# Gate and up projections of a second ffn: eight products of tiles, or seven of quarters' sums for pairs of tiles

## The chip, the cores and the metric

The kernel runs on one core of a Trainium2 chip. The metric is the device time of one execution in microseconds, as the median of several runs. TensorE does the matmuls into PSUM, VectorE (DVE), ScalarE (ACT) and GpSimd (POOL) do the rest, and transfers are issued from two queues, that of SyncE (SP) and that of GpSimd.

## The reference

Two layers over an input of 2 x 512 x 512 in float32. The first layer multiplies an autocorrelation attention with the SiLU of a first ffn. The second layer multiplies a state-space mixer (128 heads, an input projection of some 18,600 columns) with the SiLU of a second ffn. Each layer adds its product to its input. The second ffn is what the change is about; its weights are int4 values with a scale for each group of 128:

```python
def _L1_ffn_ref(x, gate_q, gate_s, up_q, up_s, down_q, down_s):   # H = 512, I = 1792, G = 128
    Wg = dequant(gate_q, gate_s)
    Wu = dequant(up_q, up_s)
    Wd = dequant(down_q, down_s)
    gate_score = jax.nn.silu(jnp.einsum('bsh,ih->bsi', x, Wg))
    intermediate = gate_score * jnp.einsum('bsh,ih->bsi', x, Wu)
    return jnp.einsum('bsi,hi->bsh', intermediate, Wd)
```

The `x` of it is the layer norm of the first layer's output, `xn1T` in the kernel (transposed, one tile of 128 x 4 x 512 for each of the two batches). The mixer also needs, ahead of its main loop, the decays of all heads (softplus, cumulated sums, exponentials) and the output projection's weights times the norm's weights.

## The kernel before, in words

The kernel has three parts in time: the first layer (to about 245 us), the second ffn (to about 574 us), and the mixer with the final products (to the end). The first layer's instructions are placed by a scheduler; from the second ffn on (`tc.manual_schedule()`) each engine runs what the program issues in the order it is written.

The second ffn goes through the 1792 inner columns in four blocks of 512, 512, 512 and 256 (`blocks`). The weights of a block come by two transfers each for gate, up and down (the values `q` and the broadcast scales `w`), and VectorE multiplies the two (`dequant`, L503) into one of six tiles of a ring. For each batch `b` and each tile `i` of 128 inner columns, TensorE makes `pg` and `pu` (L721): four matmuls of 128 x 128 weights with 128 x 512 columns for each of the two, added up over the 512 input features in one PSUM bank. A float32 matmul is two instructions in the trace, so eight for `pg` and eight for `pu`. ScalarE takes the SiLU of `pg` into `it` (L729), VectorE multiplies it by `pu` (L730). After the tiles of a batch the down projection follows, `pf` (L752), four row tiles of 128 with one matmul for each of the block's tiles, which VectorE adds into `gl` (L760, L762).

Between these tiles the program issues, one step at a time, two generators. `prepare` (`pieces`) makes what the mixer needs: loads of its small inputs, the root of the mean square (ScalarE's squares L567), `hn` and its transposes `ht` into `hT` (L580, L581), the projection `pdt` (L593), a softplus by a series on VectorE (L614 to L625), `Af` and its two parts (L628 to L636), and the sums `cs`, `cj`, `ct` by TensorE (L642 to L667), which go to memory as `cs_d`, `ea_d` and `sl_d`. `scale_out` (`scaled`) takes the output projection's weights through the core: a load of 512 KB into one of two tiles `wop` (L688, SP's queue), two multiplications by `gn` on VectorE (L697), a store to `wo_d` (L700, GpSimd's queue). A step loads piece i and scales piece i - 1:

```python
for i in range(len(pieces) + 1):
    if i < len(pieces):
        ts[i] = tmp.tile([P, WOP, D], F32, tag="wop", name=f"wop{i}", bufs=2)
        nc.sync.dma_start(ts[i], ...)
    if i > 0:
        ...                      # two tensor_scalar of 128 x 512
        nc.gpsimd.dma_start(wo_d[g][:, k : k + WOP, :], t)
    yield
```

PSUM has six banks for the second ffn's products (`bank`, tag `mm`), given out in turn, and two for transposes.

The mixer already makes its gates in another way (`Gates`, L1035 to L1107): for two tiles together, from quarters of the weights and of `hT`, by seven products of 128 x 128 with 128 x 256 for what would be eight. It needs sums of quarters of the columns (`th`, made by GpSimd once for each batch, L607) and of the weights (`sw`, L1055), and the results come together in PSUM halves and by ScalarE's copies and VectorE's additions. Steps for which `plain` is true make their gates by whole tiles (`gate`, L1026).

Of the kernel before, what the change touches and what calls it, by code (L numbers as in the profile page):

```python
# [8 lines left out]
F32 = mybir.dt.float32  # L9
# [6 lines left out]
P = 128  # L16
D = 512
# [25 lines left out]

WOP = 2
# [6 lines left out]
def fused_kernel(  # L51
# [412 lines left out]
    def hquarters(b):  # L464

        return [
            hT[:, 2 * k : 2 * k + 2, b * S + j * HD : b * S + j * HD + HD]
            for k in range(2)
            for j in range(2)
        ]  # L470
# [21 lines left out]
    with ExitStack() as l1:  # L492
# [33 lines left out]
        def prepare():  # L526
# [27 lines left out]
            for b in range(B):  # L554
# [48 lines left out]

                b11, b12, b21, b22 = hquarters(b)
                t1, t2, t3, t4 = (th[:, b, i] for i in range(4))
                for dst, p, q_ in ((t1, b12, b11), (t2, b22, t1), (t3, b22, b12), (t4, b21, t2)):
                    nc.gpsimd.tensor_tensor(dst, p, q_, ALU.subtract)  # L607
# [54 lines left out]
                csT = row("csT", "csT", (P, 2, S))  # L662
                eaT = row("eaT", "eaT", (P, 2, S))
                for j, a in enumerate((Ah, Al)):
                    ps = bank(f"ct{b}{j}")
                    for r in range(NCH):
                        nc.tensor.matmul(  # L667
                            ps[:, bass.ts(r, P)], a[:, r, :], upper, start=True, stop=True
                        )
                    nc.vector.tensor_copy(csT[:, j, :], ps)  # L670
                    nc.scalar.activation(eaT[:, j, :], ps, AF.Exp)
                nc.sync.dma_start(cs_d[b], csT[:, 0, :])
                for j in range(2):
                    nc.sync.dma_start(ea_d[j, b], eaT[:, j, :])
# [4 lines left out]
        def scale_out():  # L679

            pieces = [divmod(i, GT) for i in range(0, NG * GT, WOP)]
            ts = {}
            for i in range(len(pieces) + 1):
                if i < len(pieces):
                    g, k = pieces[i]
                    ts[i] = tmp.tile([P, WOP, D], F32, tag="wop", name=f"wop{i}", bufs=2)
                    o0 = g * GW + k * P
                    nc.sync.dma_start(  # L688
                        ts[i],
                        out_wT[o0 : o0 + WOP * P, :].rearrange("(k p) o -> p k o", p=P),  # L690
                    )
                if i > 0:
                    g, k = pieces[i - 1]
                    t = ts.pop(i - 1)
                    for j in range(WOP):
                        ct = g * GT + k + j
                        nc.vector.tensor_scalar(  # L697
                            t[:, j, :], t[:, j, :], gn[:, ct : ct + 1], None, ALU.mult
                        )
                    nc.gpsimd.dma_start(wo_d[g][:, k : k + WOP, :], t)  # L700
                yield
# [4 lines left out]
        ]  # L706
        fin = {kind: load_block(kind, 0) for kind in "gud"}
        w = {"g": fin["g"](), "u": fin["u"]()}
        pieces, scaled = prepare(), scale_out()
        for n, (i0, iw) in enumerate(blocks):  # L710
# [3 lines left out]
            for b in range(B):  # L714
                its = []
                for i in range(ni):
                    ps = {}
                    for kind in "gu":
                        ps[kind] = bank(f"p{kind}{i0}{i}{b}")
                        for k in range(KD):  # L720
                            nc.tensor.matmul(  # L721
                                ps[kind],
                                w[kind][:, k, bass.ts(i, P)],
                                xn1T[b][:, k, :],
                                start=(k == 0),
                                stop=(k == KD - 1),
                            )
                    it = hand.tile([P, S], F32, tag=f"h{4 * b + i}", name=f"it{i0}{b}{i}")
                    nc.scalar.activation(it, ps["g"], AF.Silu)  # L729
                    nc.vector.tensor_tensor(it, it, ps["u"], ALU.mult)  # L730
                    its.append(it)
                    if b == 0 and i == (2 if n == 0 else 0):
# [3 lines left out]
                    if b == 1 and i == 0 and more:  # L736
                        nxt["g"] = nxt["g"]()
                        nxt["u"] = load_block("u", n + 1)
                    if b == 1 and i == ni - 1 and more:
                        nxt["u"] = nxt["u"]()  # L740
                        fin["d"] = load_block("d", n + 1)
                    if n > 0 or b > 0:
                        next(pieces, None)
                        next(scaled, None)
                if n == 0 and b == 0:
                    wh = {q: load_hid(q) for q in range(2)}
                    wbc = {0: load_bc(0)}
                for r in range(NCH):
                    rt = b * NCH + r
                    po = bank(f"pf{i0}{rt}")  # L750
                    for i in range(ni):
                        nc.tensor.matmul(  # L752
                            po,
                            its[i][:, bass.ts(r, P)],
                            w["d"][:, i, :],
# [10 lines left out]
                    if r % 2 == 1 and (n > 0 or b > 0):  # L766
                        next(pieces, None)
                    if n > 0 or b > 0:
                        next(scaled, None)
            w.update(nxt)  # L770
# [13 lines left out]
    with ExitStack() as sm:  # L784
# [250 lines left out]
        class Gates:  # L1035
# [4 lines left out]
            def __init__(self, s):  # L1040
# [3 lines left out]
                a11, a12, a21, a22 = (  # L1044
                    w[:, 2 * k : 2 * k + 2, bass.ts(r, P)] for r in range(2) for k in range(2)
                )
                sw = wk.tile([P, 4, 2, P], F32, tag="sw", name=f"sw{s}", bufs=1)
                s1, s2, s3, s4 = (sw[:, i] for i in range(4))
                for dst, x, y, op in (
                    (s1, a21, a22, ALU.add),  # L1050
                    (s2, s1, a11, ALU.subtract),
                    (s3, a11, a21, ALU.subtract),
                    (s4, a12, s2, ALU.subtract),
                ):
                    nc.gpsimd.tensor_tensor(dst, x, y, op)  # L1055
                b11, b12, b21, b22 = hquarters(b)
                t1, t2, t3, t4 = (th[:, b, i] for i in range(4))
                self.factors = {
                    1: (a11, b11),
                    2: (a12, b21),  # L1060
                    3: (s4, b22),
                    4: (a22, t4),
                    5: (s1, t1),
                    6: (s2, t2),
                    7: (s3, t3),
                }

            def multiply(self, *which):
                for i in which:
# [7 lines left out]
                    x, y = self.factors[i]  # L1077
                    for k in range(2):
                        nc.tensor.matmul(  # L1079
                            ps,  # L1080
                            x[:, k, :],
                            y[:, k, :],
                            start=(i in (1, 2) and k == 0),
                            stop=(k == 1),
                            skip_group_check=True,
                        )
# [229 lines left out]
        def step(d):  # L1316
# [149 lines left out]
            else:  # L1466
# [12 lines left out]
                hcd = [values(s, px) for s, px in zip(n[:1], pxs)]  # L1479
# [3 lines left out]
                hcd += [values(s, px) for s, px in zip(n[1:], pxs[1:])]  # L1483
# [6 lines left out]
                if plain(d):  # L1490
                    held = [gate(a[0], "pj")]
# [179 lines left out]
```

## Time and profile before

| | |
|---|---|
| median of 7 runs | 2325.96 us (2323.52 to 2329.19) |
| the profiled execution | 2327.99 us, its span 2326.2 us, granted TensorE clock 0.992 |
| PE busy | 2273.7 us (98%) |
| DVE, ACT, POOL busy | 1406.7, 1222.6, 1067.3 us |
| second ffn, 272 to 574 us: PE, DVE, ACT, POOL busy | 296.63, 131.48, 54.87, 31.59 us of 302 |
| `pg`, `pu`, `pf` | 101.8, 100.7, 99.7 us busy, 224 instructions each |

A group's line gives the source line, the engine, the operation, written and read tiles, shapes and count; then busy us and mean ns of one; then the idle time of the engine just before the group and what ended it. A matmul's busy time is modelled and overlaps its neighbours (its mean is 592 to 599 ns for 512 columns, where one starts every 429 ns), so the pace of TensorE is read from stretches of the chain or the timeline, not from the mean. In the timeline a line gives start and length in us of a run of like instructions, and in brackets the idle time before it and its releaser.

### The profile page before, as it was taken

The numbers are of one execution on the slowest core, as the hardware profiler recorded it, in microseconds if no ns is written. First come the engines' busy times: TensorE is split into PE (matmuls) and PEld (weight loads), VectorE is DVE, ScalarE is ACT, GpSimd is POOL, SyncE is SP. The second block draws the span as 40 slices with busy tenths as digits, with TensorE's granted clock in tenths as the row PEclk, the third lists the DMA queues.
The fourth block names the chain that finished last, engine by engine and source line by source line (L and its number), as shares of the span: only waits on it lengthen the run. The fifth ranks groups of instructions, "written<-read, shape, count | busy, mean of one in ns | idle before, by whom it ended". The sixth has DMA issues, their size and how long they took to land.

```text
span 2326.2 us, 32436 instructions
## 1 busy us (share of the span) xinstructions
PE 2273.7 (98%) x11516; PEld 1547.3 (67%) x11516; DVE 1406.7 (60%) x2672; ACT 1222.6 (53%) x2605; POOL 1067.3 (46%) x907
## 2 busy tenths in 40 slices
PE   7989999999999999999999999999999999999998
PEld 4545444544557777777777777777777777777776
DVE  5263436632666666666667666666666676756663
ACT  3141112111676666666666575666666665657560
POOL 4151201100164554745554474447465654645475
PEclk9999999999999999999999999999999999999999
DMA  4012356762454444434544354545445454544452
GB/s 165 0 57 70 99 166 226 257 236 82 132 169 138 143 138 154 123 123 139 184 135 128 118 159 136 145 154 146 118 128 168 130 156 127 159 118 126 142 173 91
DMA packets 194482, 323.33 MB, mean 139 GB/s; under 512 B 16656, under 2 KB 128144, under 8 KB 191888
## 3 DMA queue, kind: packets, MB, share of 16 engines
q1 hardware_dynamic: 188432, 300.27, 42.8%
q0 software_dynamic: 5888, 20.97, 2.3%
q8 instruction: 92, 1.51, 0.3%
q14 instruction: 70, 0.57, 0.1%
HBM read 294.45 MB, written 26.74 MB: 138 GB/s over the span
## 4 chain that ended last, share of the span: by engine, by line
PE 88%; DVE 5%; ACT 3%; DMA 2%; POOL 1%; issue 1%; SPq 0%; DVEq 0%; POOLq 0%; ACTq 0%
PE pjh L873 18%; PE of L1224 14%; PE gt L1079 12%; PE py L903 5%; PE pjbc L873 5%; PE pf L752 4%; PE pn L1001 3%; PE py L912 3%; PE pu L721 3%; PE pg L721 3%; PE ofy L1224 2%; PE sh L417 2%; PE gty L1079 2%; PE px L955 2%; PE hu L306 2%; PE gt L873 1%
## 5 line engine op out<-in xcount | busy, mean ns | idle before, releaser
L873 PE MATMUL pjh<-hT,wh 128*128 128x512 f32 x1024 | 467.6, 599 | 0.5
L1019 POOL TENSOR_TENSOR eb<-CT,eb 128x768 f32<-128x768 f32 x128 | 230.1, 1818 | 455.2 <-DMA eb<-ea_d 426.2
L884 DVE SCALAR_TENSOR_TENSOR hid<-pjh,cw,hid 128x511 f32<-128x511 f32 (+2 forms) x384 | 286.7, 747 | 82.3 <-ACT hid L879 73.3
L979 ACT ACTIVATE cs<-cs,sl 128x128 f32<-128x128 f32 x1024 | 323.6, 388 | 0.8 <-DMA cs<-cs_d 0.8
L873 PEld LDWEIGHTS pjh<-hT,wh 128*128 128x128 f32 x1024 | 187.8, 190 | 202.8 <-issue 200.6
L994 DVE TENSOR_TENSOR cs<-de,CB 128x512 f32<-128x512 f32 x256 | 175.2, 684 | 76.3 <-ACT de L993 76.3
L1055 POOL TENSOR_TENSOR sw<-wg 128x256 f32<-128x256 f32 x114 | 84.1, 738 | 280.1 <-PE gt L1079 280.1
L879 ACT ACTIVATE hid<-pjh,cb,cw 128x512 f32<-128x512 f32 x128 | 99.2, 775 | 165.3 <-PE pjh L873 165.2
L993 ACT ACTIVATE de<-cs 128x512 f32<-128x512 f32 x256 | 154.0, 602 | 51.0 <-DVE cs L994 45.0
L903 PE MATMUL py<-cs,hc 128*64 128x128 f32 x2048 | 180.3, 276 | 0.0
L1238 DVE SCALAR_TENSOR_TENSOR acc<-of,rg,acc 128x256 f32<-128x256 f32 x192 | 92.0, 480 | 138.4 <-PE of L1224 137.7
L1079 PE MATMUL gt<-th,sw 128*128 128x256 f32 x684 | 175.6, 379 | 0.0
L1351 POOL TENSOR_TENSOR y<-y,sgt 128x512 f32<-128x512 f32 x124 | 161.9, 1327 | 14.9 <-ACT sgt L1107 10.4
L912 PE MATMUL py<-eb,st 128*64 128x128 f32 x1536 | 149.1, 273 | 0.0
L948 POOL TENSOR_TENSOR sums<-sums,sq 128x512 f32<-128x512 f32 x110 | 140.0, 1273 | 19.5 <-ACT sq L944 15.8
L1007 DVE SCALAR_TENSOR_TENSOR st<-st,sl,pn 128x64 f32<-128x64 f32 x512 | 103.8, 274 | 63.1 <-ACT st L1003 63.1
L1079 PEld LDWEIGHTS gt<-th,sw 128*128 128x128 f32 x684 | 126.7, 190 | 21.4 <-issue 6.5
L903 PEld LDWEIGHTS py<-cs,hc 128*64 128x64 f32 x2048 | 121.5, 137 | 15.4 <-issue 13.4
L932 DVE SCALAR_TENSOR_TENSOR y<-hid,Dcol,y 128x512 f32<-128x512 f32 x128 | 129.0, 1008 | 4.5
L1224 PE MATMUL of<-wt,y 128*128 128x256 f32 x512 | 120.6, 379 | 0.0
L873 PE MATMUL pjbc<-hT,wbc 128*128 128x512 f32 x256 | 119.5, 602 | 0.8 <-issue 0.8
L931 DVE TENSOR_TENSOR y<-py,el 128x512 f32<-128x512 f32 x128 | 87.5, 684 | 53.4 <-PE py L912 53.4
(283 smaller groups left out, 4299.7 us busy)
## 6 DMA issues: line engine op xcount, KB each, us to landing
cs<-cs_d SPq DMA_DIRECT2D x128, 512.0 KB, 4.3
eb<-ea_d SPq DMA_DIRECT2D x256, 192.0 KB, 6.2
wh<-in_in_wT SPq DMA_DIRECT2D x64, 512.0 KB, 9.2
wg<-in_in_wT SPq DMA_DIRECT2D x64, 512.0 KB, 7.6
el<-ea_d SPq DMA_DIRECT2D x256, 128.0 KB, 7.5
wop<-in_out_wT SPq DMA_DIRECT2D x32, 512.0 KB, 4.3
wo_d<-wop POOLq DMA_DIRECT2D x32, 512.0 KB, 4.7
wo<-wo_d SPq DMA_DIRECT2D x16, 1024.0 KB, 8.0
```

The costliest lines, as they stand in the source:

```text
L873: nc.tensor.matmul(ps, w_of(k), hT[:, k, bass.ts(b, S)], start=(k == 0), stop=(k == KD - 1))
L884: nc.vector.scalar_tensor_tensor(dst[:, j:], ps[:, : S - j], cw[:, ct, KCONV - 1 - j : KCONV - j], dst[:, j:], ALU.mult, ALU.add,)
L903: nc.tensor.matmul(py[bass.ts(hh, HP), bass.ts(c, P)], hc[:, c, bass.ts(hh, HP)], M[:, hh, bass.ts(c, P)], start=True, stop=(c == 0),)
L912: nc.tensor.matmul(py[bass.ts(hh, HP), bass.ts(c, P)], st[:, c - 1, bass.ts(hh, HP)], cte[:, hh, bass.ts(c - 1, P)], start=False, stop=True,)
L948: nc.gpsimd.tensor_tensor(sums[u], sums[u], q, ALU.add)
L979: nc.scalar.activation(m[:, bass.ts(c, P)], m[:, bass.ts(c, P)], AF.Relu, bias=sls[g][:, 3, b * NCH + c, h0 + hh : h0 + hh + 1], scale=-1.0,)
L993: nc.scalar.activation(pe, m, AF.Exp, scale=-1.0)
L994: nc.vector.tensor_tensor(m, pe, CBs[s // GT].rearrange("p c i -> p (c i)"), ALU.mult)
L1019: nc.gpsimd.tensor_tensor(eb_t[s], CTs[s // GT][:, P:].unsqueeze(1).to_broadcast([P, 2, S - P]), eb_t[s], ALU.mult,)
L1079: nc.tensor.matmul(ps, x[:, k, :], y[:, k, :], start=(i in (1, 2) and k == 0), stop=(k == 1), skip_group_check=True,)
L1224: nc.tensor.matmul(ps, x[:, k, :], y[:, k, :], start=(first and k == 0), stop=(k == 3), skip_group_check=True,)
L1351: nc.gpsimd.tensor_tensor(y_of(s), y_of(s), sgs.pop(s), ALU.mult)
```

## The change

The gate and up projections of a pair of tiles are made from seven products of quarters for each of gate and up, in place of the whole tiles, for all pairs but the very first (block 0, first pair, which stays as it was, `single_tiles`). `xn1T` takes the place that `hT` has in the mixer's gates, and shares `th` with it: GpSimd makes the column sums of `xn1T` after the first pair of batch 0, and those of `hT`, which the mixer reads, after the last pair. GpSimd also makes the weights' sums for each pair (`weight_sums`), four operations of 128 x 256 for gate and four for up, the third in place of a quarter of the weights. The order within a block is now pair by pair with both batches, and the down projections of both batches follow together.

`scale_out` has 64 pieces of 256 KB in three tiles, and scales piece i - 2 while it loads piece i. `side()` issues one step of `prepare` and two of `scale_out`; it comes after each half pair and after every second row tile of the down projection. The loads of `wh` and `wbc` for the mixer come later (the tiles of `wh` hold the up weights' sums until then), and `csT` and `eaT` use tiles that are already there. In the mixer, steps without `Gates` make the values of both tiles ahead of the next unit's `inner`, and the first gate of a plain step takes the bank `of` where no output is under way. What `Gates` shares with the new code went into functions (`column_sums`, `row_sums`, `seven`, `product`).

```diff
+    def seven(a, sums, columns, b):
+        a11, a12, _, a22 = row_quarters(a)
+        s1, s2, s3, s4 = sums
+        b11, _, b21, b22 = column_quarters(columns)
+        t1, t2, t3, t4 = (th[:, b, i] for i in range(4))
+        return {
+            1: (a11, b11), 2: (a12, b21), 3: (s4, b22), 4: (a22, t4),
+            5: (s1, t1), 6: (s2, t2), 7: (s3, t3),
+        }
...
         def scale_out():
-            pieces = [divmod(i, GT) for i in range(0, NG * GT, WOP)]
+            pieces = [divmod(i, GT) for i in range(NG * GT)]
...
-            for i in range(len(pieces) + 1):
+            for i in range(len(pieces) + 2):
                 if i < len(pieces):
                     g, k = pieces[i]
-                    ts[i] = tmp.tile([P, WOP, D], F32, tag="wop", name=f"wop{i}", bufs=2)
+                    ts[i] = tmp.tile([P, D], F32, tag="wop", name=f"wop{i}", bufs=3)
...
-                if i > 0:
-                    g, k = pieces[i - 1]
-                    t = ts.pop(i - 1)
+                if i > 1:
+                    g, k = pieces[i - 2]
+                    t = ts.pop(i - 2)
...
+        def pair_of_tiles(its, sums, b, name):
...
+            for kind in "gu":
+                multiply(kind, 1)
+                multiply(kind, 5)
+                nc.scalar.copy(quarter(kind, 0), ps[kind][:, 0])
...
+            for kind in "gu":
+                multiply(kind, 2)
+                nc.vector.tensor_tensor(
+                    quarter(kind, 0), quarter(kind, 0), py["gu".index(kind)], ALU.add
+                )
+            yield
+            for i, c in ((6, 1), (7, 3)):
+                for kind in "gu":
+                    multiply(kind, i)
+                    nc.scalar.copy(quarter(kind, c), ps[kind][:, 0])
+                    if i == 7:
+                        nc.vector.tensor_tensor(
+                            quarter(kind, 3), quarter(kind, 3), ps[kind][:, 1], ALU.add
+                        )
+            for kind in "gu":
+                multiply(kind, 4)
+                multiply(kind, 3)
+                nc.vector.tensor_tensor(
+                    quarter(kind, 1), quarter(kind, 1), ps[kind][:, 1], ALU.add
+                )
+            nc.scalar.activation(its[1][:, 0:HD], ps["g"][:, 0], AF.Silu)
+            nc.scalar.activation(its[1][:, HD:], its[1][:, HD:], AF.Silu)
+            nc.scalar.activation(its[0], its[0], AF.Silu)
+            for c in (2, 3, 0, 1):
+                x = ps["u"][:, 0] if c == 2 else us[c]
+                nc.vector.tensor_tensor(quarter("g", c), quarter("g", c), x, ALU.mult)
+            yield
...
+        def side():
+            next(pieces, None)
+            for _ in range(2):
+                next(scaled, None)
...
+            for q in range(ni // 2):
+                for b in range(B):
...
+                    for half in range(2):
+                        next(run)
+                        if n > 0 or q > 0:
+                            side()
...
+                    if n == 0 and q == 0 and b == 0:
+                        for s in range(B):
+                            column_sums(s, xn1T[s])
...
+                    if q == 0 and b == 0 and ni > 2:
+                        ahead = {kind: weight_sums(kind, 1, f"{i0}_1") for kind in "gu"}
...
+            if more:
+                ahead = sums = {kind: weight_sums(kind, 0, f"{i0}_2") for kind in "gu"}
+            else:
+                wh = {q: load_hid(q) for q in range(2)}
+                for b in range(B):
+                    column_sums(b, hT[:, :, bass.ts(b, S)])
+            for b in range(B):
                 for r in range(NCH):
...
-                    if r % 2 == 1 and (n > 0 or b > 0):
-                        next(pieces, None)
-                    if n > 0 or b > 0:
-                        next(scaled, None)
+                    if r % 2 == 1:
+                        side()
...
-                hcd = [values(s, px) for s, px in zip(n[:1], pxs)]
+                hcd = [values(s, px) for s, px in zip(n, pxs)]
...
-                    held = [gate(a[0], "pj")]
+                    held = [gate(a[0], "pj" if o else "of")]
```

## The prediction

> **What bounds the kernel now.** I read the clock and span first (one core, granted clock 0.992), then the page's slices and chain, then the stage of the change by windows, then TensorE's timeline in it, then the other engines' rows.
>
> ```profile
> PE 2273.7 (98%) x11516; PEld 1547.3 (67%) x11516; DVE 1406.7 (60%) x2672; ACT 1222.6 (53%) x2605; POOL 1067.3 (46%) x907
> ...
> PE 88%; DVE 5%; ACT 3%; DMA 2%; POOL 1%; issue 1%; SPq 0%; DVEq 0%; POOLq 0%; ACTq 0%
> ```
> TensorE is busy 98% of the span and 88% of the chain: matmul time taken away shortens the span unless a new wait takes its place. The second ffn runs from about 245 to 574 us. In its windows (us; then PE, PEld, DVE, ACT, POOL busy; clock, DMA share, GB/s):
>
> ```profile
> 272.00:574.00 302.00, 296.63 (x827) 143.17 (x826) 131.48 (x207) 54.87 (x89) 31.59 (x47) 0.99 0.55 188
> ```
> VectorE has 170 us free there, ScalarE 247, GpSimd 270. There is room in sum; the question is order. TensorE's timeline shows the few waits there are:
>
> ```profile
> 259.15 2.74 PE L721 MATMUL pg<-xn1T,w_g 128*128 128x512 f32 x6
> 267.34 1.94 PE L135 MATMUL xn1t<-ident,acc 128*128 128x128 f32 x8 [5.46 <-DVE acc L198]
> ...
> 341.82 2.05 PE L593 MATMUL pdt<-wdt,hT 128*128 128x128 f32 x16 [0.93 <-DVE hT L581]
> ...
> 374.95 0.77 PE L642 MATMUL cs<-Af,after 128*128 128x128 f32 x2 [3.61 <-DVE Af L628]
> ```
> After the 3.61 the instructions run at half speed (cs takes 0.43 us for two where it later takes 0.22) for 6.8 us by the clock record: 3.4 us more.
>
> **The products (gain).** Eight products of a tile pair are 16 instructions of 512 columns per kind and batch; seven products of quarters are 28 of 256. The chain of waits, merged, has rows for both sizes, unbroken:
>
> ```profile
> 2247.29 3.45 PE of L1224 x16
> ...
> 2266.66 6.87 PE gt L873 x16
> ```
> So 6.87 against 28 x 3.45/16 = 6.04: 0.83 each. Of 7 pairs, 6 change, for 2 batches and 2 kinds: 24 x 0.83 = **-20.0**.
>
> **The junction with the first ffn (loss).** The built order puts the transposes that make xn1T of batch 1 behind four groups of eight matmuls (pg, pu, pg, pu); before, the fifth group stood around them, and six of its eight ran before the wait. The release (VectorE's acc at 267.34) is not moved: TensorE is out of work at 259.15 and goes on at about 271.8 (four sets of transposes from 267.34 on, two PSUM buffers for them, ScalarE's copies of 0.59 between), one group poorer: **+3.4**. Should the copies to xn1T come sooner it is 2.7, at worst 5.
>
> **Sums on GpSimd (hidden).** Before the first seven-product pair GpSimd forms eight column sums (1.28 each by the th rows) and eight weight sums of 128x256:
>
> ```profile
> L1055 POOL TENSOR_TENSOR sw<-wg 128x256 f32<-128x256 f32 x114 | 84.1, 738 | 280.1 <-PE gt L1079 280.1
> ```
> Batch 1's column sums wait for xn1T at 271.8: 271.8 + 4 x 1.28 + 8 x 0.73 = 282.8. The cover is batch 1's plain tiles, 271.8 + 4 x 3.43 = 285.5. The spare is 2.7 us; past it every us is TensorE's. Later weight sums (5.8 us a burst) have 27 us of down projections or a whole pair as cover; the column sums of hT (10.2) have the last 13.7 us of them. Cost 0; at most 3. The later loads of wh and wbc lie beside the same projections and the 7 us of pjbc: 0.
>
> **Old waits that go.** The Af wait with its half clock (3.61 + 3.4), hT's 0.93, and the 1.6 us in which pf waited for its tile (pf of batch 0 now has batch 1's pair before it): **-9.5**. What is late next follows.
>
> **New waits.** A pair uses its PSUM halves again: product 6 waits for ScalarE's copy of 1, 7 for that of 6, 4 for that of 7, product 3 for VectorE's add behind copy 7. A copy takes 0.37, an add 0.42, a product 0.86, and one product of the other kind stands between, so alone none of it waits. But both engines run strictly in order, and each half pair is followed by preparation steps and two scalings; what is queued behind them is the next copy or add, and TensorE waits for that. TensorE comes to product 6 at 24 x 0.2156 = 5.2 us after a pair's start, to product 3 at 9.5.
> - Block 0, batch 1: ScalarE has four squares (0.62 + 0.19 each), two table loads (1.28) and a root, 6 us, ahead of the copy: 1.3; then VectorE a dequantization (2.28), two hn and four scalings ahead of the add: 2.7. Together 4.
> - Block 1, first pair: VectorE has the last gl (0.9), the series (5.04), two scalings (0.88), two adds (0.84), Af's eight steps (4.46), two scalings (0.88) ahead of the add (0.42): 13.4 against 9.5, so 4; as long as the wait that halved the clock, so 3.4 more. 7.4.
> - Block 1, batch 0, second pair: squares and root (4.7) between copies 1 and 6: 1.6.
> - Block 2: cs behind Af 1; the pieces behind the eight sl_d stores (0.76 each on SP, 6 us) 2.5.
>
> Sum **+16.5**; no row shows these pairs, so from 5 (only the ScalarE ones) to 30.
>
> **The weight pieces.** Before, two tiles of 512 KB, one place between load and scaling; after, three of 256 KB. The rows (KB each, median us to landing):
>
> ```profile
> wop<-in_out_wT SPq DMA_DIRECT2D x32, 512.0 KB, 4.3
> wo_d<-wop POOLq DMA_DIRECT2D x32, 512.0 KB, 4.7
> ...
> x_d<-x POOLq DMA_DIRECT2D x8, 256.0 KB, 2.6
> ...
> fin<-x_d SPq DMA_DIRECT2D x8, 256.0 KB, 3.9
> ```
> One call takes two places. Its second load reuses the tile whose scaling is the first of the same call, and is scaled in the next call. So from call to call must pass: scaling 0.48, to GpSimd 0.3, store, to SP 0.44, load, to VectorE 0.13, less 0.48: 0.87 + store + load. Stores of 256 KB take 2.3 to 3.2, loads 2.8 at best, 4.3 for the larger in this stage: 6.0 to 8.4. I take 2.6 + 3.4: 6.9. TensorE's pace: 20 half pairs x 6.04, 12 calls in pf x 6.87, 21.4 us of side matmuls (ht, pdt, cs, cj, ct): 224.6 us for 32 calls, 7.0 each. It just fits on average; in pairs without side matmuls it does not, and VectorE has some 3 us of slack there. **+3**, from 0 to 35. The 51.5 us that VectorE waited for wop were mostly beside TensorE's work and bring nothing back.
>
> The Trainium skill, "DMA: Bandwidth & Descriptors", section Anatomy of one DMA, speaks against cutting the pieces: a transfer costs about 2.0 us fixed plus bytes at 436 GB/s, so halving saves little. An estimate by it is 2.6 for each 256 KB, a gap of 6.1 and this term 0; the rows in this busy stage are slower, and I went by them.
>
> VectorE's scalings also meet GpSimd: two of them that take 0.88 took 1.90 beside the th sums at 352. Seven bursts at 1 us are 7 us of VectorE's time, mostly in its free time; a third is in the 3 above. The Trainium skill, "SBUF — State Buffer", section Who interferes with whom, has an exclusive lock there: whichever comes second waits for the whole instruction. By it every scaling could lose up to a sum's length, 64 x 0.73 = 47 us as an estimate if all met, which they cannot: bursts last 35 us in all.
>
> **The mixer.** In the steps of the first and last unit without seven products the first gate moves to another PSUM bank and no longer waits for conv (rows: gt behind hid, 0.59, 1.32, 0.60, 0.59): -3.1. In step 0 both tiles' values come ahead of a conv; the second pn need not wait 2.38, but the next projection then waits for that conv, until 624.1 rather than 625.39: -1.3, or -3.7 if the half clock there goes too. Together **-4.4**, from 0 to -7.
>
> **Sum.** -20.0 + 3.4 - 9.5 + 16.5 + 3 - 4.4 = **-11.0**. The profiled execution took 2327.99 (span 2326.2 and 1.8 around it), so 2317.0; it lies 2.0 above the median of the seven runs, 2325.96, so the forecast for the median is **2315**.
>
> **Rivals.**
> 1. *The saving is eaten by the order of VectorE's queue.* If the new waits are 25 rather than 16.5, or two more of them halve the clock (3.4 each), -11 becomes about -3: 2323, no difference. For: the whole sum hangs on waits that no row shows. Against: before, VectorE waited 51.5 us for pieces and TensorE lost only 9.5.
> 2. *The pieces set the pace; slower.* The mechanism is the loop store, load, scaling above; it decides once store + load passes 6.1 us. At 7.1 the gap is 8.0: 32 x (8.0 - 7.0) = 32, less some 10 of slack at both ends, and less the 3 counted: -11 + 19, 2334. For: the 512 KB rows in this stage are 4.3 + 4.7. Against: the 256 KB stores of rows nearby take 2.3 and 2.6, and the same bytes go out over about the same time.
> 3. *The waits hardly come.* With new waits of 5 and pieces 0 the sum is -25: 2301. For: the queues have much free time. Against: the block 1 queue of 13.4 us is certain.
>
> That it doesn't do what it says is no rival: the built order shows 28 short matmuls per kind and pair.
>
> **How the numbers follow.** About 0.2% (4.7 us) is what a measurement of this kernel can tell from no change. Forecast 0.58, rival 1 0.17, rival 2 0.17, rival 3 0.08. The forecast's own range, from the bounds of waits and pieces near the values taken, is 2307 to 2321. Faster: forecast and rival 3, 0.66; same 0.17; slower 0.17. The range leaves out most of rival 3 and the upper half of rival 2: 2303 to 2331.
>
> **What would show it.** After: second-ffn products of 28 instructions in 6.0 us where nothing waits; TensorE idle some 8 us before the xn1T transposes; waits of 2 to 5 us, "DVE" as releaser, at products 3 of block 0 batch 1 and of block 1; VectorE waiting for wop less than 51.5 us; the mixer's gt without waits on hid. I am wrong if product 3 waits in nearly every pair (rival 2), or if the first seven-product pair waits for GpSimd.

## Result and the profile after

The changed kernel takes 2333.09 us (median of 11 runs, 2330.65 to 2336.03), the kernel before, beside it, 2326.11 us: a ratio of 1.0028, 95% interval 1.0021 to 1.0036. It is slower by 0.3%; the forecast was 2315, faster. Its profiled execution took 2336.03 us, the longest of the eleven and 2.9 above their median; its span is 2334.3, 8.1 us more than the span before.

The page of the changed kernel, engines' busy time and the chain by engine:

```profile
PE 2262.0 (97%) x11804; PEld 1602.6 (69%) x11804; DVE 1434.5 (61%) x2766; ACT 1247.8 (53%) x2688; POOL 1133.2 (49%) x995
...
PE 88%; DVE 5%; ACT 3%; POOL 1%; issue 1%; DMA 1%; SPq 0%; DVEq 0%; POOLq 0%; ACTq 0%
```

TensorE is busy 11.7 us less and the span is 8.1 us longer, so some 20 us of new idle time stand in it. Where: from the first `pg` to the first `pjbc` ("the stage" below) it was 245.42 to 573.83 = 328.4 us, it is 245.60 to 584.83 = 339.2; from there to the end it was 1752.4 and is 1749.5. So the stage lost 10.8 us and the rest gained 2.9.

The largest of TensorE's waits in the stage, by releaser (line waited for; us in total, times, longest):

```profile
PE py L509 <- DVE it L782: 17.2, 12, 4.8
...
PE xn1t L133 <- DVE acc L196: 8.0, 1, 8.0
...
PE pg L509 <- DVE it L791: 4.0, 2, 2.7
```

`py` is product 2, L782 the addition of product 2 on VectorE. It makes TensorE wait 12 times, and there are 12 seven-product pairs. One of the last of them, with nothing else in VectorE's queue but two scalings, in TensorE's timeline:

```profile
547.09 1.03 PE L509 MATMUL py<-xn1T,w_g 128*128 128x256 f32 x4
548.70 1.13 PE L509 MATMUL py<-xn1T,w_u 128*128 128x256 f32 x4 [0.58 <-DVE it L782]
549.67 1.03 PE L509 MATMUL pg<-th,sg 128*128 128x256 f32 x4
...
552.26 1.03 PE L509 MATMUL pu<-th,w_u 128*128 128x256 f32 x4
553.34 1.13 PE L509 MATMUL pg<-th,w_g 128*128 128x256 f32 x4
554.31 1.03 PE L509 MATMUL pg<-xn1T,sg 128*128 128x256 f32 x4
```

Four instructions take 0.86 us where nothing waits. Product 2 of up starts 1.61 us behind product 2 of gate (+0.75) and the next product 0.97 behind it (+0.11); product 4 of gate starts 1.08 behind its predecessor (+0.22, too short for the list) and is followed at 0.97 (+0.11). The whole pair takes 13.26 us, not 12.07: 1.19 lost in each of 12 pairs, 14.3 us.

Where VectorE's queue is long the same place waits longer, and TensorE runs at half speed behind it:

```profile
304.38 1.03 PE L509 MATMUL py<-xn1T,w_g 128*128 128x256 f32 x4
310.23 2.08 PE L509 MATMUL py<-xn1T,w_u 128*128 128x256 f32 x4 [4.82 <-DVE it L782]
```

What stands in that queue is seen best in the first pair of block 1, on VectorE's timeline: the last six of the seven instructions of the softplus's series, then two scalings, and only then the addition of product 2:

```profile
355.01 4.32 DVE L662 SCALAR_TENSOR_TENSOR v<-v,q 128x512 f32<-128x512 f32 x6
359.26 0.87 DVE L735 TENSOR_SCALAR wop<-wop,gn 128x512 f32<-128x512 f32 x2
360.05 0.41 DVE L782 TENSOR_TENSOR it<-it,py 128x256 f32<-128x256 f32 x1
```

The junction with the first ffn, again on TensorE:

```profile
267.54 3.73 PE L133 MATMUL xn1t<-ident,acc 128*128 128x128 f32 x16 [8.04 <-DVE acc L196]
271.95 5.58 PE L816 MATMUL pg<-xn1T,w_g 128*128 128x512 f32 x8 [0.68 <-ACT xn1T L134]
277.37 3.60 PE L816 MATMUL pu<-xn1T,w_u 128*128 128x512 f32 x8
```

The pieces cost less than was feared. VectorE's wait for them fell from the first line (before) to the second (after); the others are their transfers after (KB, us to landing):

```profile
DVE wop L697 <- DMA wop<-in_out_wT: 51.5, 18, 8.8
```

```profile
DVE wop L735 <- DMA wop<-in_out_wT: 12.4, 10, 4.0
```

```profile
wop<-in_out_wT SPq DMA_DIRECT2D x64, 256.0 KB, 2.9
wo_d<-wop POOLq DMA_DIRECT2D x64, 256.0 KB, 2.6
```

The longest of these waits does reach TensorE: behind the `sl_d` stores VectorE waits 3.96 us for a piece, and product 4 for the addition queued behind it.

```profile
496.09 0.49 DVE L735 TENSOR_SCALAR wop<-wop,gn 128x512 f32<-128x512 f32 x1 [3.96 <-DMA wop<-in_out_wT]
```

### The profile page after: what moved, and what is told of

It reads as the page before. It is cut to its first block, busy times and chain, and to the rows that moved or that the text cites. A ratio compares the mean times of both kernels' runs of the same rounds, so it can differ in the third digit from the quotient of the medians.

```text
span 2334.3 us, 33414 instructions
## 1 busy us (share of the span) xinstructions
PE 2262.0 (97%) x11804; PEld 1602.6 (69%) x11804; DVE 1434.5 (61%) x2766; ACT 1247.8 (53%) x2688; POOL 1133.2 (49%) x995
## 4 chain that ended last, share of the span: by engine, by line
PE 88%; DVE 5%; ACT 3%; POOL 1%; issue 1%; DMA 1%; SPq 0%; DVEq 0%; POOLq 0%; ACTq 0%
PE pjh L1011 18%; PE of L1334 14%; PE gt L509 12%; PE py L1041 5%; PE pjbc L1011 5%; PE pn L1139 4%; PE py L1050 3%; PE pf L893 3%; PE ofy L1334 2%; PE sh L415 2%; PE pg L509 2%; PE px L1093 2%; PE gty L509 2%; PE gt L1011 2%; PE hu L304 2%; PE pu L509 2%
## 5 line engine op out<-in xcount | busy, mean ns | idle before, releaser
L736 POOL DMA_DIRECT2D wo_d<-wop x64 | 34.7, 544 | 197.9 <-DVE wop L735 197.6
```

## Experiments

A pair's loss is "own" where it stands in every pair (1.19) and "long" beyond that. The bank theory: the own waits come because product 2 of up writes the one half of a PSUM bank while VectorE reads the other half, and product 4 likewise; TensorE waits for the reader of the bank, whichever half. (In this program each bank is also one tile. No run separates the two, so "the bank" below stands for both.) The queue theory: the waits come from what stands in VectorE's queue.

| kernel | median, us | ratio to before (95%) | stage | to the end |
|---|---|---|---|---|
| changed | 2333.1 | 1.0028 (1.0021 to 1.0036) | 339.2 | 1749.5 |
| 1 additions of product 2 behind | 2331.6 | 1.0020 (1.0011 to 1.0029) | 334.9 | 1748.4 |
| 2 and addition of quarter 3 | 2321.8 | 0.9972 (0.9963 to 0.9982) | 326.1 | 1750.4 |
| 3 two banks | 2331.6 | 1.0026 (1.0017 to 1.0035) | 339.2 | 1749.2 |
| 4 no scaling | 2331.5 | 1.0023 (1.0014 to 1.0032) | 336.3 | 1748.4 |
| 5 = 2 + junction | 2303.0 | 0.9895 (0.9881 to 0.9909) | 308.6 | 1748.8 |
| 6 = 2 + split steps | 2318.0 | 0.9958 (0.9946 to 0.9971) | 322.4 | 1747.7 |
| 7 whole tiles everywhere | 2319.1 | 0.9961 (0.9949 to 0.9974) | 323.4 | 1750.3 |
| 8 old mixer | 2339.6 | 1.0048 (1.0033 to 1.0062) | 339.5 | 1753.3 |
| 9 = 2 + junction + split steps | 2303.6 | 0.9906 (0.9892 to 0.9919) | 308.7 | 1747.5 |
| 10 = 9, pieces on GpSimd | 2303.6 | 0.9908 (0.9895 to 0.9922) | 308.3 | 1748.2 |
| 11 = 9 without 2 | 2324.0 | 0.9991 (0.9982 to 1.0000) | 330.2 | 1750.9 |
| 12 = 7 + junction | 2307.5 | 0.9919 (0.9906 to 0.9933) | 313.0 | 1746.7 |
| 13 = 5, preparation outside pairs | 2294.2 | 0.9861 (0.9845 to 0.9877) | 298.0 | 1748.4 |
| 14 only addition of quarter 3 | 2330.3 | 1.0015 (1.0007 to 1.0024) | 335.6 | 1747.7 |
| 15 changed, preparation outside pairs | 2325.0 | 0.9993 (0.9983 to 1.0004) | 326.8 | 1751.3 |
| 16 = 13, pieces on GpSimd | 2295.7 | 0.9869 (0.9853 to 0.9885) | 295.9 | 1754.3 |

"Stage" and "to the end" come from one trace of each kernel. 1 to 4, 5 to 8, 9 to 12 and 13 to 16 each ran on one chip; the kernel before took 2326.9, 2327.1, 2326.3 and 2325.8 there.

**1. Additions of product 2 behind both products.**

```diff
             for kind in "gu":
                 multiply(kind, 2)
+            for kind in "gu":
                 nc.vector.tensor_tensor(quarter(kind, 0), ..., py["gu".index(kind)], ALU.add)
```

> The changed kernel, but VectorE's two additions of product 2 are issued behind both products 2, not each behind its own. In the changed kernel every one of the 12 seven-product pairs has a wait of at least 0.58 us (0.75 + 0.11 us against the plain pace) at product 2 of up, released by VectorE's addition of product 2 of gate, which reads the other half of the same PSUM bank. Theory A (one bank, two halves: TensorE may not start in a bank that VectorE still reads, whichever half): the wait at product 2 is gone in all pairs, 12 x 0.86 = 10.3 us, and what queued ahead of that addition on VectorE no longer holds TensorE there but in part later, at product 4: 2314 to 2323, about 2319. Theory B (VectorE's queue is full of preparation and scalings, and the place of the wait does not matter): the waits move to products 4 and 3 with their length, 2330 or more.

Measured 2331.56: neither number. No wait at product 2 is left, as the bank theory says, but the long ones moved to product 4, as the queue theory says:

```profile
PE pg L509 <- DVE it L792: 17.7, 6, 5.6
```

L792 is here the addition of quarter 3. It stands behind the same queue, and TensorE asks for it only 4.3 us later.

**2. And the addition of quarter 3 behind product 4.**

```diff
-                    if i == 7:
-                        nc.vector.tensor_tensor(quarter(kind, 3), ..., ps[kind][:, 1], ALU.add)
             for kind in "gu":
                 multiply(kind, 4)
+                nc.vector.tensor_tensor(quarter(kind, 3), ..., ps[kind][:, 1], ALU.add)
+            for kind in "gu":
                 multiply(kind, 3)
```

> As the run before, and besides the products 4 of gate and up come one behind the other, then the products 3; VectorE's addition of quarter 3 (which reads the half that product 5 filled) is issued behind product 4, so that product 4 no longer waits for it and product 3 does, with one product between. Theory A (bank): no wait of the 0.58 and 0.22 us kind is left in any pair, 12 x 1.19 = 14.3 us, and the place where TensorE first needs VectorE in a pair moves from 3.5 to 10.3 us behind its start, so most of the 19 us of longer waits behind VectorE's queue go too: 2302 to 2312, about 2306. Theory B (queue): the long waits stay and stand at product 3: 2318 or more.

Measured 2321.77: 9.8 us less than run 1, and faster than before. No own wait is left. Long ones are, now at product 3; the longest two are followed by half speed:

```profile
355.47 1.03 PE L509 MATMUL pu<-th,w_u 128*128 128x256 f32 x4
360.54 2.07 PE L509 MATMUL pg<-xn1T,sg 128*128 128x256 f32 x4 [4.05 <-DVE it L793]
```

Against the plain pace they sum to 3.6 (block 0), 6.7 (first pair of block 1 and the `cs` behind it), 1.5, 1.5 and 7.3 (behind the `sl_d` stores): 20.6 us. The bank theory's 2306 had taken most of them as gone, so it missed by 16.

**3. Two banks for the products 2, order as changed.**

```diff
-            two = bank(f"py{name}", (P, 2, HD))
-            py = [two[:, 0], two[:, 1]]
+            py = [bank(f"py{name}{j}", (P, 2, HD))[:, 0] for j in range(2)]
...
-                    product(py["gu".index(kind)], f[kind][i], kind == "g")
+                    product(py["gu".index(kind)], f[kind][i], True)
```

(Each of the two products now begins its own sum in its own bank.)

> The changed kernel in its own order, but products 2 of gate and up go to two PSUM banks instead of the two halves of one. Theory A (bank): product 2 of up does not wait any more although the addition stands before it in the program: 10 us less, and the queued part as when the additions are moved, 2314 to 2323. A pair now takes four of the six banks, which may bring a new wait at the next pair of up to 0.5 us, 6 us in all. Theory B (queue): the wait of product 2 stays as it is, 2333.

```profile
548.69 1.03 PE L509 MATMUL py<-xn1T,w_g 128*128 128x256 f32 x4
549.55 1.03 PE L509 MATMUL py<-xn1T,w_u 128*128 128x256 f32 x4
...
553.01 1.03 PE L509 MATMUL pu<-th,w_u 128*128 128x256 f32 x4
554.09 1.13 PE L509 MATMUL pg<-th,w_g 128*128 128x256 f32 x4
```

The same pair as above: product 2 of up follows at 0.86, product 4 still at 1.08. So what made product 2 wait is the bank it shares, not the addition's result. The time hardly moved (2331.62), for the reason seen in run 1: product 4 waits 18.8 us in six pairs.

**4. No scalings.** VectorE's `tensor_scalar` on `wop` is left out.

```diff
-                    nc.vector.tensor_scalar(t, t, gn[:, ct : ct + 1], None, ALU.mult)
```

> The changed kernel without VectorE's 64 multiplications of the output projection's weights by the norm's weights (left out; loads and stores of the pieces stay). That takes 0.96 us of VectorE's queue from each half pair. Theory A (bank): the wait of 0.58 us at product 2 of up stays in every pair, and only the longer waits shrink by 0.9 us each, some 6 us: 2326 to 2329. Theory B (queue): the waits in the pairs go nearly all, 20 to 30 us: 2303 to 2313. If the loop of store, load and scaling set the pace, it would be shorter by the scaling and the time would fall too, by more than 6 us.

2331.54, above both numbers: the 0.58 us wait stays in every pair, and of the long ones only that behind the `sl_d` stores (4.2 us) is gone, while the first pair of block 2 loses 3.2 more. So a late piece made that one wait; scalings and pieces are not what fills the queue elsewhere.

**5. Junction, on run 2.** Batch 0 of block 0 is made whole first, and the transposes for batch 1 follow the seventh group.

```diff
+            if n == 0:
+                turns.sort(key=lambda t: t[1])
...
+                    if r == 1 and kind == "g":
+                        for a in between:
+                            features(*a)
```

> The kernel with both moves in the pairs (2321.8 us), but at the junction with the first ffn batch 0 of block 0 makes all four tiles as whole tiles first, and the four sets of transposes for xn1T of batch 1 stand behind the seventh group of eight matmuls; one pair more is made of whole tiles (2 x 0.83 = +1.7 us). Theory 1 (the junction is paid in full): against its plain pace TensorE loses 8.2 + 2.7 + 1.8 = 12.7 us there, of which about 3 stay, so -8: about 2314, 2311 to 2316. Theory 2 (what follows is held by VectorE's queue and the pieces and does not begin earlier): the 8 us come back as longer waits in the pairs, 2319 or more.

2303.04, 18.7 below run 2 and 8 under the lower theory:

```profile
263.94 3.60 PE L822 MATMUL pg<-xn1T,w_g 128*128 128x512 f32 x8
267.37 1.04 PE L133 MATMUL xn1t<-ident,acc 128*128 128x128 f32 x8
268.65 1.15 PE L133 MATMUL xn1t<-ident,acc 128*128 128x128 f32 x8 [0.24 <-ACT xn1T L134]
269.63 2.74 PE L822 MATMUL pu<-xn1T,w_u 128*128 128x512 f32 x6
```

Of the 12.6 us lost there 0.4 are left; the pair that is now whole had lost 3.6 and costs 1.7 more matmul time; the remaining 3.4 of the stage's 17.5 us are shorter long waits further on, whose cause I did not follow.

**6. Smaller steps, on run 2.**

```diff
                     nc.vector.scalar_tensor_tensor(v, v, 1.0 / n, q2, ALU.add, ALU.mult)
+                    if n == 11:
+                        yield
...
                 nc.vector.tensor_copy(part(0), grouped(z))
+                yield
...
                 nc.sync.dma_start(sl_d[g], sl[:, g])
+                yield
```

> The kernel with both moves in the pairs (2321.8 us), but the preparation goes in smaller steps: the series of seven instructions in two steps (3 and 4), the step that makes Af in two, and the eight stores of sl_d one for each step. Theory 1 (the waits left at product 3 are VectorE's queue behind single long steps, and behind pieces whose loads stand behind the eight stores): the 6.1 us around the first pair of block 1 and the 7.3 us behind the stores shrink to under 4 in all: about 2312, 2309 to 2315. Theory 2 (the pieces' transfers themselves hold VectorE): the waits stay: 2319 or more.

2317.98, between the two numbers, its interval overlapping that of run 2: not settled by this run. The waits got shorter and more; some steps came to lie beside GpSimd's weight sums (two scalings each, VectorE's timeline):

```profile
362.20 0.88 DVE L739 TENSOR_SCALAR wop<-wop,gn 128x512 f32<-128x512 f32 x2
...
369.34 1.80 DVE L739 TENSOR_SCALAR wop<-wop,gn 128x512 f32<-128x512 f32 x2
```

**7. Whole tiles everywhere, all else as changed.**

```diff
-                    if n == 0 and q == 0:
+                    if True:
                         run = single_tiles(two, q, b, name)
```

(`weight_sums` and the sums of `xn1T` are gone too.)

> The changed kernel with whole tiles for every pair, so without seven products, their GpSimd sums and their copies and additions; order of pairs and batches, places of the side steps, pieces of 256 KB and mixer as changed. Theory 1 (the seven products bring 20 to 22 us of matmul time and cost 33 us of waits in the pairs, and the rest of the change costs only the junction): the waits go and the matmul time comes back, -33 + 22, and some 3 us of old waits for Af and hT come: about 2325, 2321 to 2330. Theory 2 (order, pieces and places of the side steps are what costs, and the seven products bring their 20 us): 2345 to 2353.

2319.13, 2 us under the range of theory 1: the rest of the change is a gain of 0.4%, and the seven products as placed cost 14 us. In this trace the stage's only losses are the junction's 10.9 and the 0.9 ahead of `pjbc`.

**8. Mixer as before.**

```diff
-                hcd = [values(s, px) for s, px in zip(n, pxs)]
+                hcd = [values(s, px) for s, px in zip(n[:1], pxs)]
...
+                hcd += [values(s, px) for s, px in zip(n[1:], pxs[1:])]
...
-                    held = [gate(a[0], "pj" if o else "of")]
+                    held = [gate(a[0], "pj")]
```

> The changed kernel with the mixer's two edits undone (values of the second tile behind the conv again, the first gate of plain steps in its old bank). From the first projection of the mixer to the end the changed kernel's trace is 2.9 us shorter than that of before. Theory 1 (these two edits did it): 2336. Theory 2 (it comes from the stage before, or from chance between profiles): 2333.

2339.57. The waits of `gt` on `hid` (2.8 us in four, up to 1.04) and of the second `pn` (2.38) are back; from `pjbc` to the last `ssq` the stretch is 1719.4 us, as before (1720.3), and 1714.8 in the changed kernel. The two edits did 4.6 of the 5.5 us; the rest is within what that stretch differs by from trace to trace (1712.8 to 1717.3 in the other runs but 16).

**9. Runs 5 and 6 together.** Edits as there.

> All three moves together: the additions of a pair behind both products, the transposes of xn1T behind the seventh group with batch 0 of block 0 in whole tiles, and the preparation in smaller steps. With the first two the kernel took 2303.0 us, and its waits left in the stage sum to some 13 us. Theory 1 (these are VectorE's queue behind long steps): smaller steps take 4 to 8 us of it, 2295 to 2300. Theory 2 (they are VectorE waiting for pieces and working beside GpSimd's sums, which smaller steps do not change): 2301 to 2304.

2303.58, as run 5 and in theory 2's range: smaller steps bring nothing there. Theory 2's reason does not hold by that: see runs 10 and 13.

**10. Pieces on GpSimd, on run 9.**

```diff
-                    nc.vector.tensor_scalar(t, t, gn[:, ct : ct + 1], None, ALU.mult)
+                    nc.gpsimd.tensor_scalar(t, t, gn[:, ct : ct + 1], None, ALU.mult)
```

> As the run before, but GpSimd, not VectorE, multiplies the 64 pieces by the norm's weights. Theory 1 (pieces that come late hold VectorE, and by it TensorE): VectorE no longer waits for any piece, and 3 to 5 us less than the run before. Theory 2 (GpSimd's work beside VectorE's costs VectorE more than the pieces did; its operations took 0.83 instead of 0.43 us beside weight sums): 64 more operations of GpSimd of some 1 us beside VectorE's, and GpSimd's weight sums queue behind late pieces: 3 to 20 us more than the run before.

2303.60: neither. VectorE no longer waits for pieces, but the preparation's steps, longer beside GpSimd's longer work (`Ah` takes 0.83 us, not 0.43), hold TensorE for 2.5 and 3.5 us.

**11. Run 9 with the additions in their changed places.** The edits of runs 1 and 2 are undone.

> All moves but the first: junction and smaller steps as in the two runs before, while the additions of a pair keep the changed kernel's places. Eleven seven-product pairs are left. Bank theory (products 2 and 4 wait in every pair because VectorE reads the other half of their bank): 11 x 1.19 = 13.1 us more than with the additions moved, and the longer waits at product 2 besides: 2311 to 2318. Queue theory (the places of the additions matter only where VectorE is late, and here it is less so): at most 4 us more, 2304 or less.

2324.02, 20.4 us above run 9 on the same chip, with eleven pairs: the bank theory's direction, but 6 us beyond its range. 13.1 are own waits, and the long ones grew by more than it had allowed.

**12. Whole tiles with the junction mended.** Edits of runs 7 and 5.

> The kernel with whole tiles for every pair (2319.1 us) with the transposes of xn1T behind the seventh group. No seven products, no sums of weights, no copies of quarters. The junction's 8.2 + 2.7 us go but for 1: 2308 to 2311. Beside the run with all moves this gives what the seven products are worth where they do not wait: their matmul time is 11 pairs x 1.66 = 18.3 us; if that came in full, this kernel would be 18 us longer than that one, and if the waits left eat half of it, 9 us.

2307.48, only 3.9 above run 9. The stage is 313.0 us with 312.0 busy, at full clock:

```profile
244.80:557.80 313.00, 311.98 (x882) 150.35 (x880) 150.14 (x238) 70.96 (x107) 63.98 (x91) 1.00 0.56 192
```

So of the 18.3 us of matmul time that seven products save, the waits left in run 9 eat 14.

**13. Preparation outside the pairs, on run 5.**

```diff
-                    if n > 0 or k > 1:
-                        side()
+                    if n > 0 or k > 1:
+                        side(n == 0 or not more)
...
                     if r % 2 == 1:
                         side()
+                    else:
+                        next(pieces, None)
```

(`side(False)` leaves out the step of `prepare`; the steps are cut as in run 6, and once more behind the reciprocal.)

> Additions moved and junction moved (2303.0 us), and the preparation of the mixer leaves the pairs: but for its first four steps it is issued behind the row tiles of the down projections, one step behind each, its long steps cut in two; in the pairs of blocks 1 and 2 VectorE has only its own ten operations, two dequantizations a block and the scalings. Theory 1 (what is left of the waits is preparation queued ahead of the additions): of the 14 us lost in the stage 8 to 11 go, 2292 to 2296. Theory 2 (it is late pieces, and VectorE beside GpSimd's sums): waits of 2 to 4 us stay behind the pieces, 2299 or more. In the projections TensorE may now wait for hn or Af, 1 us each.

2294.24, 1.4% under before, the fastest kernel here. In the pairs one wait is left:

```profile
343.89 1.03 PE L514 MATMUL pu<-th,w_u 128*128 128x256 f32 x4
345.36 1.13 PE L514 MATMUL pg<-xn1T,sg 128*128 128x256 f32 x4 [0.44 <-DVE it L803]
```

The stage is 298.0, 15.0 below run 12: of the 18.3 us that eleven pairs save, 15 arrive.

**14. Only the second move, on the changed kernel.** The second half of run 2's edit.

> The changed kernel, but only the second of the two moves: products 4 one behind the other and the addition of quarter 3 behind them; the additions of product 2 stay in their places. The first move alone gave 1.5 us, both 11.3. Theory 1 (both waits stand in one queue, and each catches what the other lets pass; TensorE must be free of VectorE up to product 3): the wait at product 2 stays as long as in the changed kernel, and only the 0.33 us of product 4 in each pair and its longer waits of 1.3 and 2.7 go: 2325 to 2330. Theory 2 (the second move alone brings the gain): 2323 or less.

2330.33; product 2 waits 18.6 us in 12 pairs. Either move alone lets the other wait catch what it lets pass; only both bring the gain.

**15. Preparation outside the pairs, on the changed kernel.** Edit of run 13 alone.

> The changed kernel with the preparation out of the pairs of blocks 1 and 2 as above, and nothing else changed: additions and junction as in the changed kernel. If the long waits (some 15 us and 4 us of half clock behind them) are preparation in VectorE's queue: the 0.58 us waits stay in all 12 pairs, those of block 1 (6 us) go, 2321 to 2327. If they are late pieces: 2330 or more.

2324.95: in blocks 1 and 2 no wait over 0.9 us is left in a pair, and every pair keeps at least its 0.58. The long waits of those blocks came from the preparation: from its steps in VectorE's queue and, at the last, from its eight `sl_d` stores ahead of the pieces' loads. That of block 0, whose pairs keep their steps of preparation, stays (4.83).

**16. Pieces on GpSimd, on run 13.** Edit of run 10.

> As the first of these four, and GpSimd multiplies the pieces. With the preparation in the pairs this changed nothing (2303.6 against 2303.6 us). If late pieces are what then still holds VectorE in pairs: 2 to 5 us below the first; if VectorE has slack by then, the same within 1.5 us; if GpSimd's longer queue makes the weight sums late, above it.

2295.66, the same within the runs' spread. The stage is 2.1 us shorter, and a wait of 2.7 us with half clock in the mixer's first step takes it back; why that wait came here was not followed.

## Why the prediction was wrong

Its sum beside what the traces show, in us against the plain pace:

| term | predicted | measured |
|---|---|---|
| products | -20.0 | -20.0 (0.86 for four instructions) |
| junction | +3.4 | +5.2 (7.6 before, 12.8 after) |
| GpSimd sums | 0 | 0 |
| old waits | -9.5 | -8.3 |
| a pair's own chain | 0 | +14.3 |
| queues and pieces | +16.5 and +3 | +19.6 (what is left of the stage's 10.8) |
| mixer | -4.4 | -5.5 (`pjbc` to the last `ssq`) |
| behind the last `ssq` | 0 | +2.6 |
| sum | -11.0 | +7.9 (spans: +8.1) |

**The step that failed** is the first paragraph on new waits: that product 6 waits for a copy, product 3 for an addition, "and one product of the other kind stands between, so alone none of it waits". It took the dependence half by half. Product 2 of up has no half in common with the addition of product 2 of gate, nor product 4 with the addition of quarter 3; they share the bank, and that makes TensorE wait in every pair (runs 1, 2 and 3). The trace of the changed kernel shows VectorE's additions (L782, L791) as the releasers of both. 14.3 of the 18.9 us by which the sum missed are this term. The program itself orders these waits; whether it does so for the bank or for the tile, and what the chip would do without them, no run tests.

The Trainium skill, "PSUM — Partial Sum Buffer", section PSUM bank collisions raise a hardware error, says that two engines may not touch one bank in the same partitions at once, disjoint columns included, and that the compiler puts a dependency between them. The rows agree: 0.58 us idle at least in each of 12 pairs with one bank, none with two. Weighed beforehand, it would have put this term in the sum.

**Right in mechanism:** the waits behind VectorE's queue. Predicted 19.5 with the pieces, measured 19.6 (19.5 by its rows), and 20.6 in run 2, the kernel that the prediction thought it had before it; run 2's 2321.8 misses 2315 by the other terms. That the sums agree so closely is luck. By place: block 0 batch 1, 4 against 5.8; first pair of block 1, 7.4 against 5.7; its second pair of batch 0, 1.6 against 0.6; behind the `sl_d` stores, 2.5 (and 3 for pieces) against 4.2; and 3.3 in two more pairs, where 1 was counted. And TensorE mostly met the queue at product 2 of up, 4.3 us into a pair, where I had it at product 3, 9.5 us in. Runs 13 and 15 show for blocks 1 and 2 that it is the preparation that filled it.

**Sizes.** The junction cost 1.8 more than its term, because the clock was still halved in the first `pg` behind it (5.58 us for eight, not 3.60). That looks like chance: of the ten traces with this junction it shows in five (changed, 2, 3, 8, 14) and not in the other five, where the term comes out at 3.3. Of the old waits I counted 3.4 us of half clock behind `Af`, from a record of 6.8 us that begins 1.1 us before the wait ends; in what TensorE did there it cost 2.8. The 1.6 us in which `pf` waited for its tile are a row of weight loads; TensorE's products lost 0.5 by it. The mixer came out 1.1 better than its term; the two edits are worth 4.6 by run 8, against 4.4, the half clock behind the second `pn` included. Store and load of a piece took 2.6 + 2.9 rather than 2.6 + 3.4, so the loop needs 6.4 of the 7.0 us between calls. This is nearer to the 2.6 for each that the prediction worked out from the skill's page and set aside; that page gives its fit for transfers that GpSimd issues, as only the stores are. The 2.6 behind the last `ssq` are in every other kernel's profile as well (1.6 to 4.2 over that of before, run 8 included). All of those come from the changed kernel and before has one trace, so their cause stays open.

**Hidden, as predicted:** GpSimd's last sum begins at 284.13 and takes 0.73, the first seven-product pair begins at 287.67 without a wait.

**The rivals.** The change ended slower, but not by rival 2: store and load took 5.5 us together, under the 6.1 from which it decides, and leaving the scalings out or giving them to GpSimd changed the time by no more than 1.6 us (runs 4, 10, 16). Rival 1 had the right place, VectorE, and not the mechanism: the queue's waits were no more than the forecast's. A wait in nearly every pair, which the prediction put down to rival 2 and to product 3, showed at products 2 and 4 and is neither rival's.

## What to carry to other kernels

Before a PSUM bank is split between two uses, ask who else touches the bank, not who touches the half: in this program a reader of one half holds up a matmul into the other, so issue the reads behind the matmuls that share the bank, or use two banks (at every such place: run 3, which did it at one, gained nothing). When two waits hang on one in-order queue, moving one of them only moves the idle time to the other; find the last place at which the bound engine needs that queue, and move all earlier ones behind it. A faster product chain needs the helping engines sooner: take foreign work out of their queues where the chain runs, and issue it where they idle (here from 2303 to 2294 us).

## What the runs showed of the hardware

Equal waits cost unequal clock. The junction's wait of 8.04 us is in the changed kernel and in run 7 alike; behind it eight matmuls took 5.58 us in the one and 3.70 in the other, the granted clock being 0.50 until 275.5 us in the first and 1.00 from 270.0 on in the second. In the changed kernel a wait of 2.67 us was followed at once by half speed (2.07 us for four instructions), where one of 2.79 was followed by none (1.13):

```profile
458.60 1.13 PE L509 MATMUL py<-xn1T,w_u 128*128 128x256 f32 x4 [2.79 <-DVE it L782]
...
497.74 2.07 PE L509 MATMUL pg<-th,w_g 128*128 128x256 f32 x4 [2.67 <-DVE it L791]
```

One of 3.30 (360.51) was followed by it only in part in the first product and wholly in the second, those of 0.58 never. The Trainium skill, "TensorE: Matmul & The Clock Gate", Part 1, says that the gate judges by a free-running window of some 3.4 us, so that the phase decides; these rows agree that the length alone does not.

VectorE beside GpSimd's sums of 128x256 took 0.90 for a scaling that else takes 0.44 in pairs (run 6), and GpSimd's first sum there 1.81, not 0.72. Smaller steps gained nothing, and such places may be part of the reason; no run shows it alone.
